# Smaller chunks in slabs 2, 3 and 7, three steps without layer-1 sums, and one more adjacency buffer

## The chip, the cores and the metric

The kernel runs on one core of one Trainium2 chip. The metric is the device time of one execution in microseconds; the median of several runs counts. PE is the matmul engine (PEld its weight loads), DVE the vector engine, ACT the scalar engine, POOL the GpSimd engine, SP the sync engine. A profile is of one execution; L247 is line 247 of the kernel before.

## The reference

Two graph layers on 4096 nodes with 64 features, each followed by a residual and a layernorm. adj is 4096 x 4096, ones and zeros, one entry in 256 set.

```python
# layer 0
support = x @ W0
mask = (adj != 0)
rank = cumsum(mask, axis=1);  deg = rank[:, -1:];  k = minimum(deg, 100)
pos = rank - (deg - k)
w = mask * where(pos > 0, 0.5 ** (k - pos), 0)
x = layernorm(x + w @ support + b0)
# layer 1
deg = clip(sum(adj, axis=1) + 1, 1)
h = (adj @ x + x) / deg
z = relu(concat([x, h], axis=1) @ W1 + b1)
x = layernorm(x + z / maximum(norm(z), 1e-12))
```

In layer 0 a neighbour's weight is halved for every later neighbour in its row, so the weights need the number of ones to the right of each entry.

## The kernel before

**Tiles, slabs, steps.** adj is read transposed. A slab g is 512 output rows, and there are 8 (NG). A tile (g, k) holds 512 neighbours by 512 rows as 128 partitions x 4 x 512 in bf16, 512 KB; each slab has 8 (NK), taken from k = 7 down to 0, since the ranks count from the right. A step is one tile, 64 in all; step i = 8g + (7 - k). All of adj is read once. Layer 0 needs each tile once, at its step; layer 1 needs it again, once the 512 nodes that it has as neighbours have left layer 0.

**The loads.** Eight loads are issued at the start; then step i issues the load of tile i + 8 on POOL's queue (load_next, L104), ahead of the other POOL work of that step. The tiles lie in the pool a16 of 32 buffers. A load waits until the buffer that it is to fill has been read for the last time, which is by the layer-1 sums of its former tile.

**Counting in chunks.** The tiles of a slab form chunks (sizes, L86). In the last step of a chunk, PE counts the ones of all tiles of the chunk ahead (count, L247, four matmuls for a tile, which run side by side), DVE adds the count to that of the slab so far (cs, L257 or, at a slab's start, L259), PE spreads it over the partitions (rep, L265), and ACT turns it into the starting exponent of every row (near, L267). So there is one cs, rep and near for a chunk, and it needs the last tile of the chunk ahead to have landed. Before, the chunks of slabs 0 and 1 are single tiles, slab 2 has 1, 1, 2, 2, 2, slab 3 has 2, 2, 2, 2, slab 4 has 2, 2, 4, and slabs 5 to 7 have 4, 4: 34 chunks.

**A step's order.** All five engines follow an order written out by hand (manual_schedule):

```python
            run(i, ACT)
            load_next()
            run(i, POOL)
            # count of the chunk ahead, in its last step; then weigh(g, k, nr)
            n_todo = len(todo)
            done = some_sums(i, QUOTA)
            # spread of the chunk ahead; then the gather of the step before
            run(i, PE)
            run(i, DVE)
```

weigh makes the weights of a tile's neighbours: 16 small matmuls with tri (v, L277), 16 with mine on near (L286), then one eviction of half of v on ACT (w, L293) and one on DVE (L294). The two buffers of v are both used by one step, so a step's matmuls into v wait for the evictions of the step before. gather (L304, four matmuls) multiplies the weights of the step before with x. If a counting step has issued no sums, half of its gather goes ahead of the rep.

**Layer-1 sums.** some_sums takes up to QUOTA = 4 matmuls (L313, one tile) from the list todo, in its order, if they are ready (the step of the tile has come, and i is at least 8(k + 1) + 7, when the x of its neighbours has left layer 0). The list holds the sums of 39 tiles and is empty after step 63; the sums that are in no job are made in the tail. By the list, sums are made in steps 15, 16, 23 to 26, and from 30 on in every step but 36.

**Hooks.** Layer 0's epilogue of slab g (first_hT to first_c1) is spread over the steps 8(g+1) to 8(g+1)+8; load_x, add_b0 and add_self go on POOL in the steps 8g+3, 8g+7 and 8g+12. first_c1 (L472, L475) prepares for layer 1 what comes from the node itself. The x load of a slab goes on SP's queue behind a memset on POOL.

**The tail.** After step 63 the remaining sums and layer 1's epilogue follow in an order written out by hand, to the last store.

**Small buffers.** The pool epi has two buffers for each of its tags: "hT", "y", "z", "near", and "sq", which holds has at the start and t1 in first_c1.

Of the kernel before, what the change touches and what calls it, by code (L numbers as in the profile page):

```python
# [9 lines left out]
F32 = mybir.dt.float32  # L10
BF16 = mybir.dt.bfloat16
# [4 lines left out]
ALU = mybir.AluOpType  # L16
# [7 lines left out]
P = 128  # L24
R = 512
TB = R // P
# [7 lines left out]
LN_EPS = 1e-5  # L34
L2_EPS = 1e-12
QUOTA = 4


@with_exitstack
def adj_resnorm_kernel(  # L40
# [24 lines left out]
    D = x.shape[2]  # L65
# [3 lines left out]

    PSUM = bass.MemoryType.PSUM  # L70
    const = ctx.enter_context(tc.tile_pool(name="const", bufs=1))
    a16p = ctx.enter_context(tc.tile_pool(name="a16", bufs=32))
    wp = ctx.enter_context(tc.tile_pool(name="wp", bufs=2))
    epi = ctx.enter_context(tc.tile_pool(name="epi", bufs=2))
    one = ctx.enter_context(tc.tile_pool(name="one", bufs=3))
# [7 lines left out]

    chunks = []
    for g in range(NG):
        sizes = {0: [1] * 8, 1: [1] * 8, 2: [1, 1, 2, 2, 2], 3: [2] * 4, 4: [2, 2, 4]}.get(g, [4, 4])  # L86
        k = NK
        for n in sizes:
            chunks.append([(g, k - 1 - i) for i in range(n)])
            k -= n  # L90
# [6 lines left out]
    def load_next(n=1):  # L97
        for _ in range(n):
            s = next(loads, None)
            if s is None:  # L100
                return
            g, k = s
            a = a16p.tile([P, KB, R], BF16, tag="a16", name=f"a16_{g}_{k}")
            nc.gpsimd.dma_start(out=a, in_=adjT[g, k])  # L104
            A[g][k] = a
# [5 lines left out]
    c1 = const.tile([P, NB, D], F32, name="c1")  # L111
# [36 lines left out]
    nc.vector.memset(zero, 0.0)  # L148
    eps_ln = const.tile([P, 1], F32, name="eps_ln")
    nc.vector.memset(eps_ln, LN_EPS)  # L150
    ident = const.tile([P, P], F32, name="ident")
    nc.vector.tensor_scalar(ident, dist, 0.0, None, ALU.is_equal)


    has = epi.tile([P, P], BF16, tag="sq", name="has")
    nc.vector.tensor_scalar(has, of_p, 0.0, None, ALU.is_equal)
    past = epi.tile([P, P], BF16, tag="hT", name="past")
    nc.vector.tensor_scalar(past, of_m, 0.0, None, ALU.is_lt)
# [28 lines left out]
    deg = const.tile([P, NB], F32, name="deg")  # L187
# [53 lines left out]
    near = {}  # L241

    def count(g, k, first, last):
        if first:
            cnt[g] = ps_m.tile([P, R], F32, tag="m", name=f"cnt_{g}_{k}")
        for q in range(KB):
            nc.tensor.matmul(  # L247
                cnt[g][quarters[q], :],
                lhsT=pick[:, PW - 4 * k : PW - 4 * k + Q],
                rhs=A[g][k][:, q, :],  # L250
                start=first,
                stop=last,
            )
        if last:
            new = one.tile([P, R], BF16, tag="cs", name=f"cs_{g}_{k}")
            if g in cs:
                nc.vector.tensor_tensor(new, cnt[g], cs[g], ALU.add)  # L257
            else:
                nc.vector.tensor_copy(new, cnt[g])  # L259
            cs[g] = new  # L260

    def spread(g, k):

        pr = ps_m.tile([P, R], F32, tag="m", name=f"rep_{g}_{k}")
        nc.tensor.matmul(pr, lhsT=further, rhs=cs[g], start=True, stop=True)  # L265
        near[g] = epi.tile([P, R], BF16, tag="near", name=f"near_{g}_{k}")
        nc.scalar.activation(near[g], pr, AF.Relu, bias=most, scale=-1.0)  # L267

    def weigh(g, k, nr):

        w = wp.tile([P, KB, R], I16, tag="w", name=f"w_{g}_{k}")
        v = [ps_v.tile([P, 2, R], F32, tag="v", name=f"v_{g}_{k}_{i}") for i in range(2)]
        for q in range(KB):
            for e in range(4):
                nc.tensor.matmul(  # L277
                    v[e // 2][quarters[q], e % 2, :],
                    lhsT=tri[quarters[e], :],
                    rhs=A[g][k][quarters[e], q, :],  # L280
                    start=True,
                    stop=False,
                )
        for q in range(KB):
            for e in range(4):
                nc.tensor.matmul(  # L286
                    v[e // 2][quarters[q], e % 2, :],
                    lhsT=mine[quarters[e], 4 * k + q, :],
                    rhs=nr[quarters[e], :],
                    start=False,  # L290
                    stop=True,
                )
        nc.scalar.activation(w[:, 0:2, :], v[0], AF.Relu, bias=less)  # L293
        nc.vector.tensor_scalar(w[:, 2:4, :], v[1], -STEP * MAX_NEIGH, 0.0, ALU.add, ALU.max)  # L294
        return w
# [3 lines left out]
    def gather(g, k, w, q0=0, q1=KB):  # L299
        if (k, q0) == (NK - 1, 0):  # L300
            acc0[g] = ps_a.tile([P, R], F32, tag="acc0", name=f"acc0_{g}")
        for q in range(q0, q1):
            b = k * KB + q
            nc.tensor.matmul(  # L304
                acc0[g],
                lhsT=xhl[:, b, :],
                rhs=w[:, q, :].bitcast(BF16),
                start=(k, q) == (NK - 1, 0),
                stop=(k, q) == (0, KB - 1),
            )  # L310

    def second(acc, g, b, first, last):
        nc.tensor.matmul(acc, lhsT=x1hl[:, b, :], rhs=A[g][b // KB][:, b % KB, :], start=first, stop=last)  # L313
# [12 lines left out]
    def ready(i, g, b):  # L326
        k = b // KB
        return i >= NK * (k + 1) + 7 and i >= when[g, k]

    def evict_part(g):  # L330
        acc = acc1.pop(g)
        if g in part:
            nc.vector.tensor_tensor(part[g], acc, part[g], ALU.add)
        else:
            part[g] = const.tile([P, R], F32, name=f"part_{g}")
            nc.scalar.copy(part[g], acc)

    def some_sums(i, n):

        done = None  # L340
        while n and todo and done is None and ready(i, todo[0][0], todo[0][1]):
            g, b, first, last = todo.pop(0)
            if first:
                acc1[g] = ps_a.tile([P, R], F32, tag="acc1", name=f"acc_part_{g}_{b}")
            second(acc1[g], g, b, first, last)
            n -= 1
            if last:
                done = g
        return done
# [55 lines left out]
    def first_hT(g):  # L405
        ep["hT", g] = epi.tile([P, R], F32, tag="hT", name=f"hT0_{g}")
        nc.scalar.copy(ep["hT", g], acc0[g])
# [60 lines left out]

    def first_c1(g):

        t1 = epi.tile([P, TB, D], F32, tag="sq", name=f"t1_{g}")
        nc.vector.scalar_tensor_tensor(  # L472
            t1, ep["pu", g], 1.0 / W_UP, b1_sb.unsqueeze(1).to_broadcast([P, TB, D]), ALU.mult, ALU.add
        )
        nc.vector.tensor_tensor(  # L475
            c1[:, ts(g, TB), :], t1, deg[:, ts(g, TB)].unsqueeze(2).to_broadcast([P, TB, D]), ALU.mult
        )

    hooks = defaultdict(list)
# [4 lines left out]
    def run(i, engine):  # L484
        for fn, args in hooks.pop((i, engine), []):
            fn(*args)

    for k in range(NK):
        i = when[0, k]
# [10 lines left out]
    for g in range(NG - 1):  # L500
        i = NK * (g + 1)
# [21 lines left out]
    def warm(n):  # L523

        a = A[0][NK - 1][:, 0, :]
        for i in range(n):
            nc.tensor.matmul(pi, lhsT=a[:, 0:P], rhs=a, start=True, stop=True)  # L527
# [10 lines left out]
    for c, chunk in enumerate(chunks):  # L538
        ahead = chunks[c + 1] if c + 1 < len(chunks) else []

        shares = [[]] * (len(chunk) - 1) + [ahead]
        nr = near[chunk[0][0]]
        for (g, k), share in zip(chunk, shares):
            i = when[g, k]
# [4 lines that stand above are left out]
            w = weigh(g, k, nr) if i == 0 else None  # L549
            for s in share:  # L550
                count(*s, s == ahead[0], s == ahead[-1])
            w = w or weigh(g, k, nr)
            run(i, "ACT, late")
            if i == 0:
                warm(4)
            n_todo = len(todo)
            done = some_sums(i, QUOTA)
            half = 0
            if share and share[-1] == ahead[-1]:
                if held is not None and len(todo) == n_todo:  # L560

                    half = KB // 2
                    gather(*held, 0, half)
                spread(*ahead[-1])
            if i == 0:
                warm(3)
            if done is not None:
                evict_part(done)
            if held is not None:
                gather(*held, half)  # L570
            held = (g, k, w)
            if g > 0 and k == NK - 1:
                first_hT(g - 1)
            run(i, PE)
            run(i, DVE)
# [256 lines left out]
    own(3, 6)  # L832
    last_relu(u2)
    first_c1(L)
    free(f"pu_{L}")
    last_sq(u2)
# [128 lines left out]
```

## Time and profile before

| | us |
|---|---|
| runs | 239.19, 241.07, 241.92 |
| median | 241.07 |
| profiled execution, own time | 239.26 |
| its span | 237.5 |

| engine | busy us | share of the span |
|---|---|---|
| PE | 209.7 | 88% |
| DVE | 176.7 | 74% |
| ACT | 133.5 | 56% |
| POOL | 82.7 | 35% |

The loads of adj are 64 of 512 KB each, with a median of 16.9 us from issue to landing; the DMA queue that they are on takes 72.7% of the 16 DMA engines' span. The span's own time is from the first to the last instruction, and the execution's time is somewhat longer. A matmul's listed duration overlaps the next one's: four of the sums that are listed with 380 ns each take 0.87 us in a row. Slices, waits and the timeline are in us from the start of the span; an entry in square brackets is the idle time of the engine just before the instruction and what ended it.

### The profile page before, as it was taken

Reading aid. Unit: us, or ns where it says so; the run is one execution under the profiler, and the core shown is the slowest. Engines: PE = TensorE matmul, PEld = TensorE weight load, DVE = VectorE, ACT = ScalarE, POOL = GpSimd, SP = SyncE. Lnnn points to the kernel's source line nnn. Section 1 sums busy time; section 2 is a strip of 40 time slices with the busy share of each in tenths; the row PEclk is TensorE's granted clock in tenths of the full one; section 3 lists DMA queues with packets and bytes.
Section 4 is the critical chain, followed back from the end, with each engine's and each line's share of the span. In section 5 each row is a group of like instructions: output and inputs, shape, how many; then the busy total and the mean of one; then the engine's idle time right before and its main releaser. Section 6 shows DMA issues by size and latency. Waiting matters only on the chain.

```text
span 237.5 us, 7391 instructions
## 1 busy us (share of the span) xinstructions
PE 209.7 (88%) x3123; PEld 97.0 (41%) x3166; DVE 176.7 (74%) x452; ACT 133.5 (56%) x200; POOL 82.7 (35%) x160
## 2 busy tenths in 40 slices
PE   8589979989989999999999999999799999998810
PEld 3123324333424533443345344533353354676700
DVE  5459888986885798579848965785378856779983
ACT  6068876786666657554655456455354531162492
POOL 8344584332432410311413151314071000168960
PEclk9799999999999999999999999999999999999995
DMA  6999999999999999999999899999990000000021
GB/s 201 208 214 221 215 213 214 222 214 214 222 213 214 213 220 215 215 212 214 195 181 197 158 207 189 197 160 177 178 186 5 0 3 0 3 0 25 0 88 66
DMA packets 11984, 37.33 MB, mean 157 GB/s; under 512 B 1328, under 2 KB 3504, under 8 KB 11952
## 3 DMA queue, kind: packets, MB, share of 16 engines
q0 software_dynamic: 9216, 33.56, 72.7%
q1 hardware_dynamic: 2736, 3.31, 4.4%
q8 instruction: 24, 0.39, 0.6%
q14 instruction: 8, 0.07, 0.1%
HBM read 69.37 MB, written 1.05 MB: 297 GB/s over the span
## 4 chain that ended last, share of the span: by engine, by line
PE 42%; DMA 36%; issue 8%; DVE 6%; POOL 5%; ACT 2%; ACTq 0%; POOLq 0%
DMA a<-in_adjT_dram 36%; PE acc L304 10%; PE acc_part L313 9%; PE v L277 5%; PE cnt L247 3%; PE v L286 3%; PE va L313 2%; POOL r L377 2%; POOL rn L377 2%; PE rep L265 1%; PE pi L527 1%; PE va L658 1%; PE vb L313 1%; PE ma L313 1%; PE pz L413 1%
## 5 line engine op out<-in xcount | busy, mean ns | idle before, releaser
L293 ACT ACTIVATE w<-v,less 128x1024 int16<-128x1024 f32 x64 | 71.2, 1113 | 54.2 <-PE v L286 45.5
L294 DVE TENSOR_SCALAR w<-v 128x1024 int16<-128x1024 f32 x64 | 78.2, 1222 | 22.4 <-PE v L286 20.9
L104 POOL DMA_DIRECT2D a<-in_adjT_dram x64 | 35.4, 554 | 102.1 <-PE acc_part L313 43.2
L304 PE MATMUL acc<-w,xhl 128*128 128x512 bf16 x242 | 65.9, 380 | 1.8 <-issue 1.0
L313 PE MATMUL acc_part<-a,x1hl 128*128 128x512 bf16 x130 | 36.8, 381 | 2.4 <-issue 1.8
L304 PEld LDWEIGHTS <-xhl 128*128 128x128 f16 x256 | 23.0, 98 | 32.8 <-issue 9.0
L313 PEld LDWEIGHTS <-x1hl 128*128 128x128 f16 x224 | 18.6, 98 | 30.5 <-issue 14.8
L277 PE MATMUL v<-a,tri 32*32 32x512 bf16 x1024 | 29.1, 384 | 0.8 <-ACT w L293 0.5
L247 PE MATMUL cnt<-a,pick 128*32 128x512 bf16 x256 | 21.4, 389 | 7.4 <-DMA a<-in_adjT_dram 6.7
L267 ACT ACTIVATE near<-rep,most 128x512 bf16<-128x512 f32 x34 | 23.2, 681 | 8.3 <-PE rep L265 8.3
L286 PE MATMUL v<-near,mine 32*32 32x512 bf16 x1024 | 27.4, 376 | 0.1
L257 DVE TENSOR_TENSOR cs<-cnt,cs 128x512 bf16<-128x512 f32 x26 | 17.8, 685 | 5.2 <-PE cnt L247 5.0
L277 PEld LDWEIGHTS <-tri 32*32 32x32 bf16 x1024 | 9.9, 87 | 19.5 <-issue 18.5
L377 POOL TENSOR_TENSOR rn<-ss,power 128x4 f32<-128x4 f32 (+1 forms) x5 | 6.3, 1275 | 26.4 <-DVE ss L680 26.4
L247 PEld LDWEIGHTS <-pick 128*32 128x32 bf16 x256 | 6.1, 94 | 22.5 <-issue 15.2
L265 PE MATMUL rep<-cs,further 128*128 128x512 bf16 x34 | 13.1, 386 | 1.1 <-DVE cs L257 1.0
L259 DVE CAST cs<-cnt 128x512 bf16<-128x512 f32 x8 | 5.5, 691 | 9.8 <-PE cnt L247 9.8
L232 POOL TENSOR_TENSOR a<-a,ident_b 128x128 bf16<-128x128 bf16 x32 | 12.7, 427 | 0.1
L286 PEld LDWEIGHTS <-mine 32*32 32x32 bf16 x1024 | 10.3, 87 | 3.2 <-issue 3.0
L658 PE MATMUL va<-wts,hT 128*128 128x64 f32 x64 | 8.0, 276 | 2.1 <-ACT hT L631 1.1
L209 POOL TENSOR_TENSOR xr<-c,xhl 128x256 f32<-128x256 f32 x8 | 5.3, 662 | 11.6 <-ACT xhl L207 11.5
L658 PEld LDWEIGHTS va<-wts,hT 128*128 128x128 f32 x64 | 7.6, 191 | 3.4 <-DVE hT L626 1.9
(136 smaller groups left out, 235.3 us busy)
## 6 DMA issues: line engine op xcount, KB each, us to landing
a<-in_adjT_dram POOLq DMA_DIRECT2D x64, 512.0 KB, 16.9
c<-in_x_quads_dram SPq DMA_DIRECT2D x2, 512.0 KB, 4.5
x<-in_x_dram SPq DMA_DIRECT2D x8, 128.0 KB, 7.0
out_dram<-u SPq DMA_DIRECT2D x8, 128.0 KB, 1.7
wts<-in_weights_dram SPq DMA_DIRECT2D x1, 160.0 KB, 6.8
```

The costliest lines, as they stand in the source:

```text
L104: nc.gpsimd.dma_start(out=a, in_=adjT[g, k])
L247: nc.tensor.matmul(cnt[g][quarters[q], :], lhsT=pick[:, PW - 4 * k : PW - 4 * k + Q], rhs=A[g][k][:, q, :], start=first, stop=last,)
L257: nc.vector.tensor_tensor(new, cnt[g], cs[g], ALU.add)
L267: nc.scalar.activation(near[g], pr, AF.Relu, bias=most, scale=-1.0)
L277: nc.tensor.matmul(v[e // 2][quarters[q], e % 2, :], lhsT=tri[quarters[e], :], rhs=A[g][k][quarters[e], q, :], start=True, stop=False,)
L286: nc.tensor.matmul(v[e // 2][quarters[q], e % 2, :], lhsT=mine[quarters[e], 4 * k + q, :], rhs=nr[quarters[e], :], start=False, stop=True,)
L293: nc.scalar.activation(w[:, 0:2, :], v[0], AF.Relu, bias=less)
L294: nc.vector.tensor_scalar(w[:, 2:4, :], v[1], -STEP * MAX_NEIGH, 0.0, ALU.add, ALU.max)
L304: nc.tensor.matmul(acc0[g], lhsT=xhl[:, b, :], rhs=w[:, q, :].bitcast(BF16), start=(k, q) == (NK - 1, 0), stop=(k, q) == (0, KB - 1),)
L313: nc.tensor.matmul(acc, lhsT=x1hl[:, b, :], rhs=A[g][b // KB][:, b % KB, :], start=first, stop=last)
L377: nc.gpsimd.tensor_tensor(r, v, power[:, 0:n], ALU.pow)
L658: nc.tensor.matmul(pz[:, t, :], lhsT=h[:, ts(b % TB, P)], rhs=wn_sb, start=True, stop=True)
```

## The change

- The chunks of slab 2 are single tiles, slab 3 has 1, 1, 2, 2, 2, and slab 7 has 2, 2, 4: 39 chunks in place of 34.
- In the steps 23, 26 and 28 no layer-1 sums are made. The list is as before, so the sums of steps 23 to 26 are made in 24, 25, 27 and 29, and from step 30 on the same step makes the same sums.
- The pool a16 has 33 buffers.
- first_c1 works in place in c1 rather than through t1, which empties the tag "sq" with has moved to the tag "y"; ident, a constant that is read at the start alone, moves to a buffer of the tag "near".

```diff
+SAVED = 23, 26, 28
...
-    a16p = ctx.enter_context(tc.tile_pool(name="a16", bufs=32))
+    a16p = ctx.enter_context(tc.tile_pool(name="a16", bufs=33))
...
-        sizes = {0: [1] * 8, 1: [1] * 8, 2: [1, 1, 2, 2, 2], 3: [2] * 4, 4: [2, 2, 4]}.get(g, [4, 4])
+        sizes = {3: [1, 1, 2, 2, 2], 4: [2, 2, 4], 7: [2, 2, 4]}.get(g, [1] * 8 if g < 3 else [4, 4])
...
-    ident = const.tile([P, P], F32, name="ident")
+    ident = epi.tile([P, P], F32, tag="near", name="ident")
...
-    has = epi.tile([P, P], BF16, tag="sq", name="has")
+    has = epi.tile([P, P], BF16, tag="y", name="has")
...
-        t1 = epi.tile([P, TB, D], F32, tag="sq", name=f"t1_{g}")
+        t1 = c1[:, ts(g, TB), :]
         nc.vector.scalar_tensor_tensor(
             t1, ep["pu", g], 1.0 / W_UP, b1_sb.unsqueeze(1).to_broadcast([P, TB, D]), ALU.mult, ALU.add
         )
         nc.vector.tensor_tensor(
-            c1[:, ts(g, TB), :], t1, deg[:, ts(g, TB)].unsqueeze(2).to_broadcast([P, TB, D]), ALU.mult
+            t1, t1, deg[:, ts(g, TB)].unsqueeze(2).to_broadcast([P, TB, D]), ALU.mult
         )
...
-            done = some_sums(i, QUOTA)
+            done = some_sums(i, 0 if i in SAVED else QUOTA)
```

## The prediction

> **What bounds the kernel now.** I read the page's slices first.
>
> ```profile
> span 237.5 us, 7391 instructions
> PE   8589979989989999999999999999799999998810
> PEclk9799999999999999999999999999999999999995
> DMA  6999999999999999999999899999990000000021
> GB/s 201 208 214 221 215 213 214 222 214 214 222 213 214 213 220 215 215 212 214 195 181 197 158 207 189 197 160 177 178 186 5 0 3 0 3 0 25 0 88 66
> ```
>
> One slice is 237.5/40 = 5.94 us. For 19 slices, to about 113 us, the transfers run at 201 to 222 GB/s without a pause; then the rate falls to 158 to 207, although a third of adj is still to come, and stops near 178 us. PE is full from slice 5 to the tail but for slice 27 (the 7). So there are two stages: to about 109 us the transfers set the pace, after that PE does. The full clock means that only waits and work matter.
>
> Next, who waits for a transfer (columns: total us, times, longest), for the whole span and then, in the second fence, for 100 to 193 us alone.
>
> ```profile
> POOL a L104 <- PE acc_part L313: 43.2, 19, 9.7
> POOL a L104 <- DMA a<-in_adjT_dram: 29.2, 19, 2.2
> PE cnt L247 <- DMA a<-in_adjT_dram: 6.7, 8, 2.6
> ```
> ```profile
> PE cnt L247 <- DMA a<-in_adjT_dram: 1.7, 1, 1.7
> ```
>
> In the second stage PE loses to transfers in one place. The timeline of PE shows it, and the POOL timeline shows the load that was late:
>
> ```profile
> 165.24 0.83 PE L247 MATMUL cnt<-a,pick 128*32 128x512 bf16 x12
> 167.72 0.40 PE L247 MATMUL cnt<-a,pick 128*32 128x512 bf16 x4 [1.65 <-DMA a<-in_adjT_dram]
> 168.05 0.43 PE L277 MATMUL v<-a,tri 32*32 32x512 bf16 x16
> ```
> ```profile
> 95.06 0.53 POOL L104 DMA_DIRECT2D a<-in_adjT_dram  x1 [9.73 <-PE acc_part L313]
> 159.70 0.53 POOL L104 DMA_DIRECT2D a<-in_adjT_dram  x1 [2.10 <-PE acc_part L313]
> ```
>
> This is step 55 (counting from 0), which counts the four tiles of the chunk ahead, 56 to 59. Three are there; tile 59 was issued at 159.70, only after the layer-1 sums of step 52 gave its buffer back, and needed 8.0 us to land (the DMA issues in that window), so until 167.7. In steps 39, 43, 47 and 51 the same order holds by a little: by issue time plus time to landing, the fourth tiles are in at 119.2, 130.9, 142.7 and 154.3 us, when their count starts about 119.9, 131.9, 142.9 and 154.9: margins of 0.2 to 1.0 us.
>
> **The change, part by part.** Durations are from the profiled execution of 239.26 us (span 237.5, so 1.76 outside it).
>
> *Slab 7 in 2, 2, 4.* Step 55 now counts 56 and 57, issued at 150.35 and 153.68 and long there; 58 and 59 are counted at step 57, near 170 us, when 59 has been in since 167.7 even if its load is no earlier. Without a wait, v follows the first of sixteen count matmuls by 0.98 (142.17 to 143.15 at step 47), so step 55's v would stand at 165.24 + 0.98 = 166.22, not 168.05: **-1.83**. Eight of the sixteen counts move to step 57, which is no change in sum. The added chunk costs a cs (DVE 0.685), a rep and a near (ACT 0.681). On PE a rep takes 0.22 until the next matmul starts (74.72 to 74.94, 97.78 to 97.99): **+0.22**. The cs lies under the four sums (0.87) and the near under the rest of step 57, which is 3.3 us long; both engines are about half busy there (172 to 176 us: DVE 3.51, ACT 3.00 of 4; 176 to 180: 2.97 and 1.11). Without that cover it would be 0.685 + 0.681 = 1.4 more.
>
> *The 33rd buffer.* I worked out by hand which step's sums free which buffer. Before, the load of tile L, issued in step L - 8, needs the sums of step L - 7 (the load of step 52, tile 60, goes at 162.11 behind the sums of step 53); with one more buffer it needs those of L - 8. So each load from 38 on goes a step, 2.4 to 3.3 us, earlier, and POOL's wait of 9.73 before tile 38 shrinks by about 3. This removes no further PE wait, as there is none, but turns the margins of 0.2 to 1.0 into about 3. In this execution: 0. POOL's hooks that queue behind the loads (load_x, add_b0, add_self, and SP's x loads behind the memset) only come earlier.
>
> *Slab 2 in singles, slab 3 in 1, 1, 2, 2, 2.* Four more chunks: 4 x 0.22 = 0.9 on PE, 2.7 each on DVE and ACT. In exchange PE no longer waits for the second tile of a pair (0.37 at 57.89, 0.61 at 68.30). The template is slab 1, which has singles under the same layer-0 work: from step 9 to step 15, v goes from 35.54 to 51.30, 15.8 for six steps. Step 17 then starts at 57.12 + 0.33 = 57.45 and step 23 at about 73.2, against 73.48. *SAVED* moves four sums each from steps 23, 24, 25, 26 to 24, 25, 27, 29; the number before step 30 is the same. Step 25 needs tile 27, which is in at 78.5 (tile 35's load waits for it until 78.61), so its v stands no earlier than 78.9, against 79.30. From there: step 25 3.5 as before, 26 and 28 without sums 2.2 to 2.65 (the row of step 28 is 87.76 to 90.41), 27 and 29 with sums and a rep about 2.6, where the sums fill the wait for cs. That puts step 30 at 92.0 to 93.3, against 92.77. The end of this stage is not set by it: step 35 counts tile 39, which lands at 98.24 + 10.7 = 108.95 out of a transfer stream that has not paused, and its sixteen counts take 1.33 in place of 1.05 because of that. PE has 0.28 to spare there and can't gain beyond it. So **0**, with bounds of 0 and +1.0 (all four reps on the path and the lower pair of step lengths missed).
>
> [...]
>
> *Memory edits.* first_c1 writes c1 in place: the same two DVE operations (0.34 + 0.42). ident in the tag "near" and has in "y" make a later near wait for readers of ident; the last of them ends at 8.03 us and the first near comes after the first count at 8.97. Cost 0; the cover is the 7.70 us of the first load, and without it the cost is one 0.23 cast.
>
> The tail from 193 us is untouched. **Sum:** -1.83 + 0.22 = -1.6, so 239.26 - 1.6 = 237.65 for an execution like the profiled one. The runs are 239.19, 241.07 and 241.92: the profiled one is like the fastest, and the median is 1.81 above. The trace can't say where that comes from. What is in the transfer stream before 109 us stays; what is in the four margins goes, since a landing 1 us later stalls before but not after. I let a third stay, 0.6: **238.2 us**.
>
> **Rivals.**
> (A) *The late load moves to step 59.* Step 59 still counts four tiles; tile 63 is in at 172.83 + 6.1 = 178.9, and PE would now be there at 179.9 - 1.6 = 178.3. If the buffer release gave no lead, 0.6 is lost again: 238.2 + 0.6 = 238.8. The rates below 200 GB/s with DMA nearly full speak for a slower stream; the freed step speaks against.
> (B) *All of the runs' spread is of margins.* Then the median falls to the profiled run's sum or a little under, 237.0 to 237.6. For it: margins of 0.2.
> (C) *The spread is all elsewhere*: 241.07 - 1.6 = 239.5, no change to be told.
> (D) *Slower: the count's own chain sets slab 2 and 3.* Where sums are taken away, or DVE and ACT are full, PE has only half a gather to cover cs, rep and near (0.69 + 0.38 + 0.68 = 1.75). If four chunks pay that in full, 7.0, less the pair waits of 0.98 and the spare 0.28, PE comes 5.7 late to step 35 and the time is 241.07 - 1.6 + 5.7 = 245.2; half of it gives 242.3. It decides from 1.6 + 0.28 = 1.9 late at step 35. For it: slab 1 has stretches with DVE 4.00 of 4 and a near wait of 0.49 at 50.97. Against: slab 1 kept up with the transfers all the same.
> (E) *The 33rd buffer doesn't bring loads forward* (the releases stay a step late): as A.
>
> **Chances and range.** Forecast 0.40, B 0.17, A with E 0.13, C 0.18, D 0.12. The likeliest time is 238.2. Its own range is 237.0 to 239.3; B reaches down to 236.5, C and A up to 239.5, the weak half of D to 242.3. I take 236.4 to 241.0. One per cent, about what a measurement of this kernel can tell from no change, is 2.4 us: faster means under 238.7. Forecast and B are mostly there, A half: 0.55. Slower than 243.5 is the strong half of D: 0.08. The rest, 0.37, is within 1%.
>
> **What would show it.** In the changed profile: no wait of cnt for DMA near 165 us, and v of steps 55 to 63 about 1.6 earlier; loads 38 on issued one step earlier, GB/s above 200 for longer after 113 us, and stopping earlier; step 35's v still at 109.4 and its count still delayed by tile 39. Wrong would be: v of step 30 after 93.3 and of step 35 after 110 (D); a wait at step 59 (A); loads behind the same sums as before (E).

## The result and the profile after

The median is 239.81 us (238.27 to 241.28, 22 runs) against 240.09 us of the kernel before (238.16 to 242.84, 22 runs). The ratio is 1.0004 with a 95% interval of [0.9979, 1.0028]: no change. The medians are of all runs, while the ratio is of the fast runs alone and leaves out the slowest runs of before (241.92 and more), so it is not simply 239.81 / 240.09. The profiled execution took 239.75 us, so it is like the median; its span is 238.0 us, against 237.5 before.

The page's slices after the change (the same lines as were shown of before; the line DMA is left out):

```profile
span 238.0 us, 7425 instructions
...
PE   8689979889997999999999999999999999996920
...
PEclk9799999999999999999999999999999999999795
...
GB/s 200 209 216 220 212 213 212 222 215 213 220 213 215 214 222 213 212 213 218 218 208 186 193 206 185 187 178 183 196 77 3 3 0 0 3 1 23 3 88 66
```

Slices are counted from 0. The 7 of PE that the wait at step 55 left in slice 28 is gone. The rate stays above 200 GB/s for two slices more and the transfers end half a slice earlier. But the clock, which before was full from slice 2 until the last slice, now has a 7 in slice 37 (220 to 226 us), and PE has more work in slice 38 (2 against 1). PE's waits for loads between 100 and 193 us, and its timeline at steps 35 and 55:

```profile
PE cnt L248 <- DMA a<-in_adjT_dram: 0.5, 1, 0.5
```
```profile
109.34 0.40 PE L248 MATMUL cnt<-a,pick 128*32 128x512 bf16 x4 [0.51 <-DMA a<-in_adjT_dram]
109.67 0.43 PE L278 MATMUL v<-a,tri 32*32 32x512 bf16 x16
165.92 0.61 PE L248 MATMUL cnt<-a,pick 128*32 128x512 bf16 x8
166.46 0.43 PE L278 MATMUL v<-a,tri 32*32 32x512 bf16 x16
```

Step 55 counts eight matmuls (two tiles) and waits for nothing; step 35 still waits for tile 39. The loads on POOL, tiles 38 and 59, that were issued at 95.06 after a wait of 9.73 and at 159.70 before:

```profile
92.19 0.53 POOL L105 DMA_DIRECT2D a<-in_adjT_dram  x1 [4.40 <-PE rep L266]
157.66 0.53 POOL L105 DMA_DIRECT2D a<-in_adjT_dram  x1 [2.86 <-PE rep L266]
```

Both go a step earlier. So the loads and the waits moved as they were meant to, and the time is the same. To find where the gain went, I cut the span at the first v of step 54 and of step 63, the last step of layer 0's matmuls (us; "tail" is from v of step 63 to the end of the span; e1 to e8 are the experiments below):

| kernel | v of 54 | v of 63 | 54 to 63 | tail | span |
|---|---|---|---|---|---|
| before | 162.60 | 190.38 | 27.78 | 47.1 | 237.5 |
| after | 163.28 | 189.56 | 26.28 | 48.4 | 238.0 |
| e4, before again | 163.60 | 191.17 | 27.57 | 47.1 | 238.3 |
| e1, slab 7 alone | 163.37 | 189.80 | 26.43 | 47.1 | 236.9 |
| e2, slabs 2, 3, SAVED alone | 163.79 | 193.15 | 29.36 | 47.1 | 240.2 |
| e3, 33rd buffer alone | 163.38 | 189.32 | 25.94 | 48.4 | 237.8 |
| e6, after with 32 buffers | 164.79 | 191.38 | 26.59 | 47.1 | 238.5 |
| e7, memory edits, 32 buffers | 163.01 | 190.67 | 27.66 | 47.1 | 237.8 |
| e8, after, a16 shifted | 164.04 | 190.32 | 26.28 | 48.4 | 238.8 |

The span grew by 0.5 = +0.68 (to step 54) - 1.50 (54 to 63) + 1.33 (tail). The first term is within what one execution of the kernel before differs from the next (162.60 and 163.60). The tail's 1.33 is not: the tail is 47.1 in each kernel with 32 buffers of this table and 48.4 in each with 33.

The tail's timeline before, where slab 3 enters layer 1's epilogue (L679 and L680 are the square sums of slab 2 and their maximum with a floor, L702 on POOL the residual of slabs 0 and 1, L626 hT of slab 3, L658 its last_pz, L607 the sums for the first half of slab 7):

```profile
217.21 0.41 DVE L679 TENSOR_REDUCE ss<-u 128x4 f32<-128x256 f32 x1
217.65 0.16 DVE L680 TENSOR_TENSOR ss<-ss,least 128x4 f32<-128x4 f32 x1
217.72 1.27 POOL L702 TENSOR_TENSOR u<-u,x 128x512 f32<-128x512 f32 x1 [0.98 <-DVE ss L679]
219.29 0.66 DVE L626 TENSOR_TENSOR hT<-ma,part 128x512 f32<-128x512 f32 x1
220.00 1.55 PE L658 MATMUL va<-wts,hT 128*128 128x64 f32 x12 [1.02 <-DVE hT L626]
221.39 3.66 PE L607 MATMUL vb<-a,x1hl 128*128 128x256 bf16 x32
```

And after (lines one higher):

```profile
216.40 0.41 DVE L680 TENSOR_REDUCE ss<-u 128x4 f32<-128x256 f32 x1
216.62 1.27 POOL L703 TENSOR_TENSOR u<-u,x 128x512 f32<-128x512 f32 x1 [0.69 <-DVE u L698]
216.84 1.07 DVE L681 TENSOR_TENSOR ss<-ss,least 128x4 f32<-128x4 f32 x1
219.39 0.65 DVE L627 TENSOR_TENSOR hT<-ma,part 128x512 f32<-128x512 f32 x1
220.09 2.32 PE L659 MATMUL va<-wts,hT 128*128 128x64 f32 x12 [1.94 <-DVE hT L627]
222.21 4.58 PE L608 MATMUL vb<-a,x1hl 128*128 128x256 bf16 x32
```

The same instructions in the same order on each engine. Before, the maximum on 128 x 4 numbers takes 0.16, and POOL's add starts 0.07 after the maximum has started. After, POOL's add starts ahead of the maximum, which takes 1.07 and ends when the add is through (217.91 against 217.89). hT of slab 3 is 0.9 later by that, PE waits 1.94 rather than 1.02, and then the same matmuls take 2.32 rather than 1.55 and 4.58 rather than 3.66. The windows of the changed kernel show why (columns: PE, PEld, DVE, ACT and POOL busy us with counts, then the granted PE clock, DMA share, GB/s):

```profile
217.30:220.70 3.40, 1.46 (x13) 1.13 (x12) 3.40 (x23) 0.37 (x1) 2.66 (x4) 1.00 0.00 0
220.70:224.10 3.40, 3.40 (x18) 2.87 (x18) 3.05 (x22) 1.79 (x6) 3.15 (x6) 0.50 0.00 0
```

From 220.7 to 224.1 PE has half its clock. Two things are thus in the tail's loss: DVE held behind POOL, and the clock. The experiments take the change apart first, then these two. Each experiment's ratio is to runs of the kernel before that were made along with it; their medians go from 239.67 to 240.44, so between experiments the ratios say more than the times.

### The profile page after: what moved, and what is told of

The parts are those of the page before. It is cut to its first block, busy times and chain, and to the rows that moved or that the text cites. A ratio compares the mean times of both kernels' runs of the same rounds, so it can differ in the third digit from the quotient of the medians.

```text
span 238.0 us, 7425 instructions
## 1 busy us (share of the span) xinstructions
PE 211.8 (89%) x3128; PEld 98.4 (41%) x3171; DVE 180.1 (76%) x457; ACT 136.2 (57%) x205; POOL 83.3 (35%) x160
## 4 chain that ended last, share of the span: by engine, by line
PE 47%; DMA 34%; issue 7%; DVE 7%; POOL 2%; ACT 2%; ACTq 0%; POOLq 0%
DMA a<-in_adjT_dram 34%; PE acc L305 11%; PE acc_part L314 10%; PE v L278 5%; PE cnt L248 4%; PE v L287 3%; PE va L659 2%; PE va L314 2%; PE vb L608 2%; PE pi L528 2%; PE rep L266 1%; PE vb L314 1%; PE ma L314 1%; PE pz L414 1%; ACT w L294 1%
## 5 line engine op out<-in xcount | busy, mean ns | idle before, releaser
L105 POOL DMA_DIRECT2D a<-in_adjT_dram x64 | 35.8, 560 | 97.0 <-PE rep L266 34.4
L314 PE MATMUL acc_part<-a,x1hl 128*128 128x512 bf16 x132 | 37.3, 381 | 2.1 <-issue 1.4
L268 ACT ACTIVATE near<-rep,most 128x512 bf16<-128x512 f32 x39 | 26.6, 682 | 8.2 <-PE rep L266 8.1
L258 DVE TENSOR_TENSOR cs<-cnt,cs 128x512 bf16<-128x512 f32 x31 | 21.2, 685 | 6.4 <-PE cnt L248 6.3
L266 PE MATMUL rep<-cs,further 128*128 128x512 bf16 x39 | 15.0, 385 | 1.0 <-DVE cs L258 1.0
L659 PE MATMUL va<-wts,hT 128*128 128x64 f32 x64 | 8.8, 292 | 2.4 <-DVE hT L627 1.9
L659 PEld LDWEIGHTS va<-wts,hT 128*128 128x128 f32 x64 | 8.4, 206 | 3.7 <-DVE hT L627 2.8
L668 ACT ACTIVATE u<-u 128x256 f32<-128x256 f32 (+1 forms) x5 | 2.5, 502 | 12.4 <-DVE u L664 12.4
```

The lines of the kernel that those rows point to most:

```text
L659: nc.tensor.matmul(pz[:, t, :], lhsT=h[:, ts(b % TB, P)], rhs=wn_sb, start=True, stop=True)
```

## The experiments

**The parts of the change.** e1: slab 7 in 2, 2, 4 as the one edit to the kernel before.

```diff
-4: [2, 2, 4]}.get(g, [4, 4])
+4: [2, 2, 4], 7: [2, 2, 4]}.get(g, [4, 4])
```


> Only slab 7's chunks of 2, 2, 4 are added to the kernel before; all else is as before. Theory 1 (won at step 55, given back in the tail): no wait of cnt for DMA at step 55, v of step 63 about 1.5 us earlier than 190.4, but PE idle near 218 to 220 us is longer than 1.0 and the time moves by 0 to -0.8 us. Theory 2 (the wait at step 55 is a chance of the one profiled execution of before): v of step 63 within 0.4 of other executions of before, time unchanged. Theory 3 (slabs 2 and 3 cost what slab 7 wins): the time is 1.2 to 1.6 us below the kernel before, since slabs 2 and 3 are untouched.

Measured: 239.11 us, ratio 0.9960 [0.9928, 0.9993]; no wait at step 55, tail 47.1. Slab 7 wins its time here, and the tail takes nothing back.

e2: the chunks of slabs 2 and 3 and SAVED, without the other edits.

```diff
+SAVED = 23, 26, 28
...
-sizes = {0: [1] * 8, 1: [1] * 8, 2: [1, 1, 2, 2, 2], 3: [2] * 4, 4: [2, 2, 4]}.get(g, [4, 4])
+sizes = {3: [1, 1, 2, 2, 2], 4: [2, 2, 4]}.get(g, [1] * 8 if g < 3 else [4, 4])
...
-done = some_sums(i, QUOTA)
+done = some_sums(i, 0 if i in SAVED else QUOTA)
```


> Only the chunks of slabs 2 and 3 and the three steps without sums; 32 buffers, slab 7 in 4, 4. Theories 1 and 2: step 35 is set by tile 39's landing, v there 109.3 to 109.8, time within 0.4 us of before. Theory 3: v of step 39 is 0.5 us or more later than in executions of before and the time is 0.6 to 1.5 us longer.

Measured: 239.95 us, 1.0003 [0.9974, 1.0033]. Its profiled execution was the slowest of its twelve (242.35). In it the count's chain does come onto PE's path once (at 70.61 the rep waits 1.21 for cs); v of step 30 stands at 94.44 and v of step 35 at 110.48, 1.4 and 0.8 later than in e4. Two late loads follow, 1.76 at step 55 and 1.29 at step 59. The median shows no cost and no gain.

e3: the 33rd buffer and the memory edits, without the smaller chunks and SAVED.

```diff
-a16p = ctx.enter_context(tc.tile_pool(name="a16", bufs=32))
+a16p = ctx.enter_context(tc.tile_pool(name="a16", bufs=33))
...
-t1 = epi.tile([P, TB, D], F32, tag="sq", name=f"t1_{g}")
+t1 = c1[:, ts(g, TB), :]
...
```


> Only the 33rd buffer with the edits that make room for it. Theory 1: tile 59 is issued a step earlier, the wait at step 55 falls from 1.65 to under 0.3 with chunks of four, v of step 63 about 1.6 us earlier, time 0 to -0.8 us as for slab 7 alone. Theory 2: nothing moves. Theory 3: -1.2 to -1.8 us.

Measured: 239.42 us, 0.9964 [0.9926, 1.0002]. From step 54 to 63 it is the shortest of all, 25.94 with chunks of four: the 33rd buffer takes away the wait at step 55 by itself. And it has the long tail.

e4: the kernel before, profiled once more.

> The kernel before once more, for a second profile. Theory 1: cnt waits 1 to 2 us for tile 59 at step 55 again, v of step 63 near 190.4, and the tail from there to the end takes 47.1 us, give or take 0.3, if DVE goes ahead of POOL at the sums' maximum, or over 48 if not. Theory 2: no such wait, or under 0.5, and v of step 63 near 189.

Measured: 240.05 us, tail 47.1, waits for loads of 0.51 at step 51 and 1.13 at step 55 in place of one of 1.65. The late load is in both executions, but not at one place.

**Is the tail's loss of the edits or of the buffers?** e5 moves hT of slab 3 ahead of the moments of slabs 4 and 5 on DVE, in the changed kernel:

```diff
     last_add(u01)
+    last_hT(3)
     last_mv(u45)
...
-    last_hT(3)
```


> The changed kernel with last_hT(3) moved on DVE ahead of the moments of slabs 4 and 5. Theory 1 (PE's gain is given back in the tail, where POOL's add of slabs 0 and 1 gets in ahead of DVE's ss maximum, hT of slab 3 comes 0.9 late, PE idles 1.9 and its clock halves for 3.4 us): PE's idle time at last_pz(3) falls from 1.9 to under 0.9, the clock stays full there, the tail from v of step 63 falls from 48.4 to 47.0 to 47.4 and the time is 0.8 to 1.4 us below the changed kernel's 239.8. Theory 2 (the tail's end is set by DVE's own work, PE's idle is harmless): tail over 48, time as the changed kernel. Theory 3 (slabs 2 and 3 cost it): tail may fall but v of step 63 is no earlier than with slab 7 alone.

Measured: 239.29 us, 0.9998 [0.9965, 1.0032]. Two lines of its PE timeline:

```profile
218.84 1.55 PE L659 MATMUL va<-wts,hT 128*128 128x64 f32 x12 [0.39 <-DVE hT L627]
...
226.39 0.66 PE L659 MATMUL va<-wts,hT 128*128 128x64 f32 x4 [2.50 <-ACT hT L632]
```

The wait shrinks to 0.39 and the clock stays full past the place where it was halved (1.00 from 216 to 228), but the next step of the chain, ACT's copy of hT for the first half of slab 7, is queued behind other work on ACT: the wait moves there. The tail is 47.9, and the median shows no gain.

e6: all smaller chunks and SAVED, with 32 buffers and the memory as before.

```diff
-a16p = ctx.enter_context(tc.tile_pool(name="a16", bufs=33))
+a16p = ctx.enter_context(tc.tile_pool(name="a16", bufs=32))
```


> All of the chunks and the three steps without sums, but 32 buffers and the memory as before. Theory 1 (the memory edits cost the tail): wait of last_pz(3) for hT 1.0, tail 47.1, time 239.0 to 239.4, as with slab 7 alone. Theory 3 (slabs 2 and 3 cost what slab 7 wins): tail 47.1 but time 239.8 to 240.4.

Measured: 239.14 us, 0.9970 [0.9938, 1.0002], tail 47.1. A late load now stops PE at step 47:

```profile
145.01 0.40 PE L248 MATMUL cnt<-a,pick 128*32 128x512 bf16 x4 [1.84 <-DMA a<-in_adjT_dram]
```

e7: the memory edits alone, 32 buffers.

```diff
-ident = const.tile([P, P], F32, name="ident")
+ident = epi.tile([P, P], F32, tag="near", name="ident")
...
-has = epi.tile([P, P], BF16, tag="sq", name="has")
+has = epi.tile([P, P], BF16, tag="y", name="has")
...
-t1 = epi.tile([P, TB, D], F32, tag="sq", name=f"t1_{g}")
+t1 = c1[:, ts(g, TB), :]
...
```

> The edits that make room (first_c1 in place, ident in near, has in y) with 32 buffers, chunks and sums as before; ident out of the constants puts the a16 buffers at multiples of 4096 bytes, where they were 512 past one. If the buffers' places decide who gets in first, POOL's add or DVE's ss maximum: wait of last_pz(3) 1.9, tail 48.4. If the 33rd buffer does: wait 1.0, tail 47.1. The wait at step 55 stays at 1.2 to 1.9 either way.

e8: the changed kernel, with the pool of small tiles opened ahead of a16, so that a16 begins at another address.

```diff
+    small = ctx.enter_context(tc.tile_pool(name="small", bufs=5))
     a16p = ctx.enter_context(tc.tile_pool(name="a16", bufs=33))
...
-    small = ctx.enter_context(tc.tile_pool(name="small", bufs=5))
```


> The changed kernel with the pool small opened ahead of a16, which puts the a16 buffers 2720 past a multiple of 4096 and changes nothing else. If their places decide: wait of last_pz(3) 1.0, tail 47.1, time 0.8 to 1.3 us below the changed kernel's 239.8. If not: wait 1.9, tail 48.4, time as the changed kernel.

Measured: e7 239.55 us (a single run) with a tail of 47.1; e8 240.16 us, 1.0004 [0.9966, 1.0042], tail 48.4. So the long tail goes with the 33rd buffer, not with the memory edits or where the pool begins.

**Another order on DVE.** In the next three, the square sums of slab 2 go ahead of the y of slabs 0 and 1. POOL's add of slabs 0 and 1 needs that y, so it can't get ahead of the maximum any more.

```diff
     own_half(1, 6)
+    last_ss(u2)
     last_y(u01)
     own_half(1, 7)
-    last_ss(u2)
```

e9 is the changed kernel with this order.

> The changed kernel with 33 buffers, and in the tail only: DVE's square sums of slab 2 (reduce and maximum) go ahead of its y of slabs 0 and 1, so POOL's add of slabs 0 and 1, which needs that y, can't start before the maximum. Theory T (the tail's lost 1.3 us are DVE's maximum held behind POOL's add): no maximum longer than what is left of POOL's add of slabs 4 and 5 (under 1.0, and it ends before 217), hT of slab 3 within 0.2 of where 32 buffers have it relative to the step 63, PE waits 1.0 at last_pz(3) and not 1.9, matmuls of last_pz(3) 1.55 and not 2.32, the sums of the first half of slab 7 3.66 and not 4.58, from v of step 63 to the end 46.9 to 47.2 and not 48.4; span 238.0 - 1.3 = 236.7, time 238.5, ratio to the kernel before about 0.995. Rival R (the 33rd buffer slows the tail in some way that this order doesn't touch): from v of step 63 to the end 48.4 again, time 239.8, ratio 1.000. Rival S (the wait moves to another engine, as it did with hT first): between, 47.8, time 239.2.

e10 has 33 buffers and slab 7 in 2, 2, 4, but slabs 2 and 3 and the sums as before.

> 33 buffers, the memory edits and slab 7 in 2, 2, 4, with slabs 2 and 3 chunked and the sums spread as before, and the same order in the tail (square sums of slab 2 ahead of y of slabs 0 and 1). Theory T: the tail is 46.9 to 47.2; v of step 63 stands as in the run of the 33rd buffer alone or the whole change, 189.3 to 189.6, so the span is 236.4 to 236.7 and the time 238.2 to 238.5, ratio about 0.994. Rival (slabs 2 and 3 and the saved steps are worth something once the wait at step 55 is gone): v of step 63 later than 190.0 here and this kernel 0.4 or more behind the one with the whole change. Rival R: tail 48.4, time 239.6.

e11 has 32 buffers and slab 7 in 2, 2, 4.

> 32 buffers, slab 7 in 2, 2, 4 as the one edit to the kernel before, and the same order in the tail (square sums of slab 2 ahead of y of slabs 0 and 1). Here the tail was already 47.09, with the maximum at 0.16. Theory T: the order has nothing to win back, the tail stays 46.9 to 47.2, the span at 236.9 and the ratio where slab 7 alone had it, 0.996. If instead the new order shortens the tail in itself, by the 1.76 of the y of slabs 0 and 1 that now waits for POOL's add of slabs 4 and 5, PE's wait of 1.02 at last_pz(3) falls by up to 0.6 and the tail to 46.5. If the maximum is now held behind POOL's add of slabs 4 and 5 instead, hT of slab 3 is later by up to 0.5 and the tail 47.6.

| kernel | us (runs) | ratio to before | 54 to 63 | tail | span |
|---|---|---|---|---|---|
| e9 | 238.56 (237.99 to 239.81) | 0.9961 [0.9928, 0.9995] | 26.28 | 46.9 | 236.6 |
| e10 | 238.26 (238.06 to 238.52) | 0.9937 [0.9908, 0.9966] | 26.28 | 46.9 | 236.3 |
| e11 | 238.76 (237.79 to 240.77) | 0.9957 [0.9920, 0.9994] | 26.27 | 47.2 | 236.3 |

The timeline of e10:

```profile
215.28 0.55 DVE L680 TENSOR_TENSOR ss<-ss,least 128x4 f32<-128x4 f32 x1
216.57 1.27 POOL L702 TENSOR_TENSOR u<-u,x 128x512 f32<-128x512 f32 x1 [0.77 <-DVE st_l L386]
218.62 1.55 PE L658 MATMUL va<-wts,hT 128*128 128x64 f32 x12 [0.58 <-DVE hT L626]
```

The maximum is held for 0.55 only, until POOL's earlier add (slabs 4 and 5) ends, and the y of slabs 0 and 1 is no longer held at all (0.68, where it took 1.76 before and after). The tail's loss is gone: the change with this order is 1.4 us shorter in span than the change alone. In e11, which had nothing to win back, PE's wait at last_pz(3) also fell to 0.58, but PE then waits 1.64 for ACT at last_pz(7a) rather than 1.10, and the tail is 47.2. The slabs 2 and 3 of e9 give nothing over e10.

**The hold or the clock?** e12 is e10 without the new order, to see the loss come back.

> 33 buffers, the memory edits and slab 7 in 2, 2, 4; slabs 2 and 3, the sums and the order of the tail as in the kernel before. It is the kernel that ran 238.26 without the new order in the tail. Theory T (the order on DVE and POOL in the tail is what costs): v of step 63 at 189.3 to 189.6, the maximum held for 1.07 behind POOL's add, PE waiting 1.9 at last_pz(3), from v of step 63 to the end 48.4, span 237.8 and time 239.5. Rival (it is slabs 2 and 3 with the saved steps that upset the tail or cost the time, and the new order only helps there): maximum 0.16, tail 47.1, span 236.5 and time 238.3 as with the new order.

Measured: 239.68 us (238.71 to 241.75), 0.9982 [0.9948, 1.0017], 1.4 above e10, or 1.1 by the ratios. But its profiled execution, span 237.1, was one of the shorter, and it misses both expectations:

```profile
217.14 1.06 DVE L680 TENSOR_TENSOR ss<-ss,least 128x4 f32<-128x4 f32 x1
220.40 1.55 PE L658 MATMUL va<-wts,hT 128*128 128x64 f32 x12 [1.94 <-DVE hT L626]
221.78 3.66 PE L607 MATMUL vb<-a,x1hl 128*128 128x256 bf16 x32
```
```profile
216.00:219.50 3.50, 2.46 (x22) 1.85 (x19) 3.46 (x17) 0.37 (x1) 2.51 (x3) 1.00 0.01 2
219.50:222.90 3.40, 2.50 (x23) 2.39 (x24) 3.37 (x26) 0.32 (x1) 2.88 (x5) 1.00 0.00 0
```

The maximum is held and PE waits 1.94, yet the clock stays at 1.00 and the tail is 47.3: the hold (of DVE's maximum behind POOL's add) alone costs 0.2, since PE later waits 0.48 for ACT's hT where it waited 1.11 before. The clock is then the rest, 1.1 to 1.2. When it falls looks like a matter of phase. In the changed kernel the stretch at half clock is 3.41 us long (220.67 to 224.08), and in each trace that shows several changes of the clock they lie whole multiples of that apart (after: 12.46, 220.67, 224.08 and 230.91; 220.67 - 12.46 = 208.21, which is 61 x 3.413), at another phase in each execution. I call a stretch of 3.41 us between two such borders a window. In the changed kernel the wait of 1.94 lay in one window; in e12 a border, at 219.43 by that spacing, splits it into halves of 0.97.

The runs without a profile point the same way. Each run also tells its mean granted clock. In three kernels with the hold the runs with a mean of 0.983 or more are about 1.0 faster than those with 0.970 to 0.975: the changed kernel 239.05 (median of 7 runs) against 240.00 (7), e3 238.43 (5) against 239.52 (5), e12 238.84 (3) against 239.78 (3). In kernels without the hold or the late loads, or with the wait filled (e1, e9, e10, e11, e13, e16), the same difference is between -0.4 and 0.5. It is a rough sign, as the mean also counts low clock at the start and the end of a run (before: 0.50 from 8.6 to 12.0 and from 230.5 on). That the clock is halved behind a window with half or more of it idle, as the next two expectations have it, was an estimate of mine from one place in two traces: from 217.3 to 220.7 PE was idle for 1.94 in the changed kernel, with the clock at 0.50 next, and for 1.02 in the kernel before, with 1.00 next. Three runs test the phase directly.

e13: the changed kernel, with PE given work in its wait.

```diff
+        for i in range(busy):
+            nc.tensor.matmul(pz, lhsT=x1hl[:, 0, :], rhs=A[L][7][:, 0, half_rows[0]], start=True, stop=True)
...
-    last_pz(u3)
+    last_pz(u3, 12)
```


> The changed kernel, and in the tail PE runs 12 further matmuls of 128x256 (results not used) between its last sums of the second half of slab 7 and last_pz(3), so some 1.3 of its wait of 1.94 there is filled with work and about 0.6 is left. DVE's order is not touched: the maximum is still held 1.07 behind POOL's add and hT of slab 3 as late as before. Theory K (the tail's loss is the halved PE clock, which is granted over windows of 3.41, and is halved after a window in which PE was idle for half or more; the hold by itself costs 0.16): the clock stays 1.00 to the end of PE's work, last_pz(3) takes 1.55 and the sums of the first half of slab 7 3.66, from v of step 63 to the end 47.2 to 47.3, span 236.8, time 238.6, ratio 0.995. Rival H (the hold of DVE costs by itself, the clock is a side show): maximum 1.07, hT of slab 3 late, and the tail still 48.0 or more, time 239.5.

Measured: 238.86 us (238.37 to 239.52), 0.9943 [0.9916, 0.9970], tail 47.25.

```profile
216.91 1.06 DVE L683 TENSOR_TENSOR ss<-ss,least 128x4 f32<-128x4 f32 x1
218.07 1.47 PE L658 MATMUL va<-a,x1hl 128*128 128x256 bf16 x12
220.16 1.55 PE L661 MATMUL va<-wts,hT 128*128 128x64 f32 x12 [0.62 <-DVE hT L627]
221.55 3.66 PE L608 MATMUL vb<-a,x1hl 128*128 128x256 bf16 x32
```

DVE is held as in the changed kernel and hT is as late; twelve useless matmuls give back 1.2 us of the tail, and the interval of the ratio lies below that of the changed kernel. That the clock is the price, and not the hold, is shown by this.

e14: e1 (32 buffers, no hold) with two useless reduces on DVE ahead of hT of slab 3.

```diff
     last_mv(u45)
+    spare = small.tile([P, 2 * TB], F32, tag="mv_37", name="spare")
+    nc.vector.tensor_reduce(spare, u45[2][1], AX.X, ALU.add)
+    nc.vector.tensor_reduce(spare[:, 0:2], u45[2][1][:, 0:2, :], AX.X, ALU.add)
```


> The kernel before with slab 7 in 2, 2, 4 (32 buffers; it ran 239.11 with a tail of 47.09), and two reduces on DVE (0.68 and 0.29, results not used) ahead of hT of slab 3: DVE's maximum is not held (0.16), but PE waits 1.02 + 0.9 = 1.9 at last_pz(3) as with 33 buffers. Theory K: the PE clock is halved for 3.41 in an execution where the wait falls into one window and not where it is split over two; by chance some 57 in 100 executions (windows of 3.41, a wait of 1.94, half a window 1.71: (3.41 - 1.94 + 2 x 0.23) / 3.41). The tail of the profiled one is then 48.4 or 47.2, and the time rises by about 0.6 x 1.2 + 0.2 = 0.9 at the median, to 240.0. Rival B (the halved clock belongs to the 33rd buffer or its layout): clock full, tail 47.1 to 47.3, time 239.1 to 239.3.

Measured: 240.30 us (238.04 to 242.84), ratio 0.9968 [0.9924, 1.0012], too wide to tell from e1's 0.9960. In the profiled execution PE waits 1.95, split by a border at 219.52 into 0.76 and 1.19; clock full, tail 47.2. That agrees with the windows, but it is one execution and does not exclude the rival; e12 does, in part, since it has 33 buffers and a full clock.

e15: the changed kernel, where the tail's tile of slab 2 takes its buffer ahead of those of slabs 0 and 1.

```diff
+    u2 = unit(2)
     u01 = unit(0, 1)
...
-    u2 = unit(2)
```


> The changed kernel with one edit: the tail's tile of slab 2 takes its buffer of the pool a16 ahead of the two tiles of slabs 0 and 1, so these three lie in other buffers; orders and work are the same. Theory L (whether POOL's add may start during DVE's reduce depends on which buffers the two read): the maximum may be back at 0.16 and PE's wait at 1.0, tail 47.1. Rival N (it does not depend on these buffers): maximum 1.07 and wait 1.94 as in the changed kernel; the tail is then 47.2 or 48.4 by where the clock's window falls.

Measured: 240.37 us (a single run), tail 48.4. The wait lies 1.6 in one window, and the clock is halved in the next:

```profile
217.34 1.07 DVE L681 TENSOR_TENSOR ss<-ss,least 128x4 f32<-128x4 f32 x1
222.00 5.32 PE L608 MATMUL vb<-a,x1hl 128*128 128x256 bf16 x32
```
```profile
219.00:222.40 3.40, 1.79 (x16) 1.76 (x17) 3.40 (x31) 0.08 (x1) 2.76 (x4) 1.00 0.00 0
222.40:225.80 3.40, 3.40 (x18) 2.44 (x17) 3.16 (x20) 2.98 (x9) 3.15 (x6) 0.50 0.02 5
```

So these buffers are not what lets POOL start early. What does is still open. In every profiled execution with 32 buffers POOL's add starts 0.43 to 0.45 after the y that it needs, with 33 buffers 0.14 to 0.15 after, also under the new order (e11 0.44, e10 0.14). DVE's maximum comes 0.36 after that y: between the two. The orders are equal, and the traces show no difference in what the add waits for: it is the same two semaphores. (The bracket at POOL's add names L679 before and the y after, but under the new order it names L386 with 32 buffers and with 33, and the 0.3 is there all the same.) What the traces do show is that POOL runs three more semaphore instructions ahead of the tail in every kernel with 33 buffers, 225 instructions in all against 222; whether that matters was not tested.

**Which part is worth having?** e16: the 33rd buffer and the memory edits with the new order, all chunks and sums as before.

> 33 buffers and the memory edits, all chunks and sums as in the kernel before, and in the tail the square sums of slab 2 ahead of the y of slabs 0 and 1. Theory M (the 33rd buffer by itself takes away the wait for loads after 113 us, so the smaller chunks of slab 7 only add their 0.3): no wait of a count for a load of more than 0.5 after 113, from v of step 54 to v of step 63 25.9 to 26.0 where the same kernel with slab 7 in 2, 2, 4 has 26.28, from v of step 63 to the end 46.9, span 236.1 and time 237.9 to 238.1. Rival O (the smaller chunks of slab 7 are what keeps the runs together): a wait of 0.5 or more at step 55 or 59 in the profiled run, or a median of 238.6 or more with runs spread over more than 2 us, where the kernel with both had 238.26 and 0.46.

Measured: 237.85 us (237.53 to 238.74, 12 runs), 0.9945 [0.9919, 0.9970]; 25.95 from step 54 to 63, tail 46.9. The profiled execution was the slowest of its runs (238.74, span 236.6). It has the lowest median here, and beats the kernel before; the changed one stands at 1.0004 of before, so it beats that by 0.9945 / 1.0004, some 0.6%. The smaller chunks of slab 7 are not needed with 33 buffers; in the profiles they cost 0.33 (26.28 - 25.95), too little to show between the ratios of e16 and e10 (0.9937).

## Why the prediction was wrong

**The step that failed is "The tail from 193 us is untouched".** The program of the tail is; its time is not: +1.33, 0.2 of it from the hold and the rest from the halved clock. The 33rd buffer was costed ("In this execution: 0") for its loads alone; the memory edits' "Cost 0" stood (e7). That one more buffer would let POOL's add come 0.3 earlier, ahead of DVE's maximum, was in no rival. The profile of before held the warning: POOL's add and the maximum started within 0.07 of each other (217.72 and 217.65), a y had already been held to 1.76 behind POOL's add just before, and PE was waiting for that very chain (1.02 at 220.00).

**Slab 7, the wait: right.** Predicted -1.83; the wait's place is free in e3, and 54 to 63 goes from 27.78 to 25.94, -1.84. But I gave it to slab 7, and nothing to the 33rd buffer. Either does it alone (e1, e3), so their gains don't add; that did not matter to the sum. (The 7 that the prediction read in slice 27 stands in slice 28.)

**The added chunk: right in kind, too small.** +0.22 predicted, 26.28 - 25.94 = +0.34 measured. So -1.6 was predicted for slab 7 in all, and 54 to 63 fell by 1.50.

**The loads: right.** Tile 38 and 59 go a step earlier, POOL's wait of 9.73 shrinks to 4.40 (I said by 3, it is 5.3), and no count after step 35 waits.

**Slabs 2 and 3 and SAVED: right.** 0, with v of step 30 at 92.92 (92.0 to 93.3 was said) and of step 35 at 109.67, still set by tile 39. e2's median is 1.0003 of before. Rival D's chain is real: in e2's slowest execution, the profiled one, it cost 1.21 at 70.61, and v of steps 30 and 35 (94.44, 110.48) passed both marks that were set for D. In the median it decides nothing. The added cs cost the loads' issues little: on POOL the 64 of them take 35.8 us in sum with five more cs, and 35.4 before.

**The offset of 0.6: too small, and the base too high.** The 241.07 that the gain was counted from came from three runs; 22 runs have 240.09, so 1.0 of the forecast fall of 2.9 was never there. And the profiled execution of before, 239.26, was a low one, 0.8 under that median. With the tail mended, the change stands at 238.56 (e9) or 238.86 (e13), 0.4 to 0.7 above the 238.2 of the forecast. In the profiles that remainder lies ahead of step 54 (v at 163.38 in e9, 162.60 before), so it belongs to this term.

**The rivals.** A fell: no wait at step 59. E fell: tiles 38 and 59 go a step earlier. C came near the right time, 239.5 and no change, by luck: its mechanism, a gain of 1.6 under a spread that stays, did not happen, as the gain came and was spent in the tail. Of B's spread, part was late loads (e4: other steps, other lengths); with them gone and the tail's clock safe the runs lie within 0.5 to 1.8 us of each other (e10 0.5, e13 and e16 1.2, e9 1.8), against 4.7 before.

## What to carry to other kernels

A stage whose program isn't changed can still change its time: look for two engines whose instructions start within some tenths of a us of each other and where one takes longer behind the other (here 1.07 in place of 0.16), above all where the matmul engine waits behind them. Price a wait of PE by what it does to the clock as well as by its length (here 1.1 to 1.2 against 0.2), and look for it in the granted clock just behind the wait; where the clock falls, put work into the wait (e13: tail 47.25 in place of 48.4), or let what it waits for go first (e9: 46.9). When two edits cure the same wait, try each alone: here one of them was only a cost.

## What the runs showed of the hardware

- **The clock.** A PE wait of 1.94 us in the tail cost 1.3 in the changed kernel, where it lay in one window of 3.41 us (half the clock behind it, tail 48.4), and 0.2 in e12, where a border splits it (clock 1.00, tail 47.3). A window with 1.61 idle (e15: 1.79 of 3.40 busy) was followed by half the clock, one with 1.40 idle (e5, 221.9 to 225.3) was not. But idle time alone doesn't decide, nor does the "half or more" of the expectations: e6's wait of 1.84 at step 47 lay in one window (143.18 to 146.59 by the same spacing), and four sums in the next took 1.04 (at 148.78) as four ahead of the wait did (at 140.28); in before PE was idle for 1.81 from 165.62 to 169.03 around step 55, and the clock was 1.00 behind it. What is different there was not tested.
- **VectorE and GpSimd.** A DVE operation on 128 x 4 numbers took 0.16 where no add of POOL was running at its start (before, e1, e14) and 1.06 or 1.07 behind POOL's add (after, e3, e12, e13); y on 128 x 512 took 0.68 in e10 and 1.76 behind the add of slabs 4 and 5 in before; the reduce ahead of the maximum took 0.41 in before and after. How the add holds the others the rows don't show, and none of them explains the 0.3 us that decided who was first.
